# A graph-convolution kernel: loads and results issued from ScalarE, other places for the weight tiles and the packs' stores, and other PSUM buffers

## The chip, the core and the metric

The kernel runs on one core of one Trainium2 chip. The core has TensorE (PE; its weight loads are shown as PEld), VectorE (DVE), ScalarE (ACT), GpSimd (POOL) and SyncE (SP), each with an instruction stream of its own, executed in order. An engine that needs another's result waits on a semaphore. Transfers are issued from an engine's stream and run on 16 shared DMA engines. SyncE does nothing here but issue transfers. The time is the device time of one execution in microseconds, the median of several runs.

## The reference

There are 50,000 nodes with 160 features each (64 scalars s, and 32 vectors v of three components) and 1,650,000 edges, sorted by their destination; 50,000 of these are the loops from each node to itself. Each edge has four numbers sh = (e0, e1).

```python
ss, vv = (s[src], v[src])
e0, e1 = sh[:, 0:1], sh[:, 1:4]
dot = jnp.einsum('eui,ei->eu', vv, e1)
out0 = C0 * (ss * e0 @ W1 + dot * INV3 @ W2)
p3 = (ss @ W3)[:, :, None] * e1[:, None, :] * INV3
p4 = jnp.einsum('eui,uw->ewi', vv * e0[:, :, None], W4) * INV3
p5 = jnp.einsum('eui,uw->ewi', jnp.cross(vv, e1[:, None, :]), W5) * INV6
out1 = C1 * (p3 + p4 + p5)
m_agg = jax.ops.segment_sum(concat(out0, out1), dst, num_segments=n)
h = concat(m_agg_scalars @ Ws * LIN_S, m_agg_vectors @ Wv * LIN_V)
x = layernorm(x + (x + relu(h)))
```

All is linear in the features of the source node. So the kernel sums, for each node, the outer products of its edges' four numbers with the 160 source features, and multiplies the sums once by a combined weight.

## The kernel before

**Units, groups, pairs.** 128 edges make a unit, 6 units a group, 2 groups a *pair*: 12 units. There are 2,087 groups, so 1,044 pairs, and the outer loop at the end of the function runs over these. For each unit GpSimd issues one gather (L349): 128 rows of 640 bytes of x, chosen by the edges' sources, into one slot of the tile `xg`. `xg` holds a pair and has four buffers, so GpSimd can be four pairs ahead. The gathers stand in order of GpSimd's own stream and wait for the buffer they write.

**The weight tile.** For a pair VectorE builds `hot` (L358, which of 32 neighbouring destinations an edge has) and from it `ha` (L361, `hot` times the four numbers of the edge, 12 units of 128 columns) in `spread`. TensorE multiplies `ha` by the gathered rows (L386, in `group_sums`; each unit gives two weight loads and two matmuls) and adds the six units of a group in PSUM, in `ps`: 128 rows (4 numbers x 32 destinations) by 160 features for each of the two groups. `ps` has two buffers in the pool `psA`.

**Turning.** `turn_sums` transposes `ps` on VectorE into `sums` (L398) and adds it into `ring` (L405), the sums of the nodes of a segment of 512 nodes, at a place that is read into a register. When a segment begins, what two segments share is added (L402).

**The order of a pair.** The loop body issues the gathers of pair p and then walks the 12 units. After the matmuls of unit 1 comes `turn_sums` of pair p - 1; after those of unit 3 comes `spread` for pair p + 1; after every unit a bit of the tasks that are waiting (`work`) and some steps of the current pack. The program fixes this order on SyncE, TensorE, VectorE and ScalarE (`manual_schedule`).

**Tasks.** `after_pair(p, f)` hands a task over when pair p has been written. For a block of 128 nodes whose last group is in pair p: `do_ahead` at p loads `xt`, the block's own rows of x, two blocks with one transfer (L644); `do_block` at p + 2 multiplies the ring by the combined weight (L704, ten matmuls into `phb`, in the pool `psM`, tag "misc") and ends with relu, residual and statistics on VectorE (L182, L184, L186); `do_root` at p + 3 takes the root on ScalarE (L191, `rstd`); `do_store` at p + 4 takes the reciprocal and scales on VectorE (L195, L196); `do_send` at p + 6 stores two blocks (L784). There are 391 blocks, one in 2.7 pairs.

**Loads of edges.** 20 groups (10 pairs) form a chunk s. `load(s + 1)` is issued at the first pair of chunk s, `place` runs four pairs later: VectorE and TensorE find the first destination of each group (L318, L320, L322), transpose indices and numbers (L326 to L331) and make `si`, `rel` and `pk`, which `gather` and `spread` read. For the first 100 groups the edges are read from the inputs (L263 to L265). For all others they come from the tensor `edges` in DRAM (L257), from which the kernel has removed the loops.

**Packs.** That removal is the work of 16 packs of up to 128 rows of 790 edges. A pack is a list of steps: read the rows (L474 to L478), three empty steps, begin (copies on ScalarE, L482 to L484), counting and marking on VectorE with a copy by ScalarE (L502), shifting by predicated copies (L566), four empty steps, and 17 stores. A store step reads 16 addresses from SBUF into registers of SyncE and issues up to 16 transfers of 18.5 KB to `edges` and as many of 0.5 KB, the loops' numbers, to `selves` (L618). A pack has 77 steps, and the loop deals them evenly over the pairs from the end of the pack before to the pack's due time. The due times, by the planner, are the pairs 38, 99, 159, 229, 289 and so on to 989; the first pack begins at pair 2.

**The loops' share.** For each segment `ask_own` loads, six pairs before the segment begins, the nodes' own rows four times over (`xr`, L675, 640 KB) and their loops' numbers (`sr`, L676), twice 256 nodes a segment; `set_own` multiplies them and transposes them into the ring (L689, L693) at two pairs before.

**Queues.** In this version `dq` is SyncE, and every transfer of the main loop but the gathers is issued there: loads, packs' reads, packs' stores, xt, xr, sr and the results. An issue that has to wait holds up those after it.

Of the kernel before, what the change touches and what calls it, by code (L numbers as in the profile page):

```python
# [39 lines left out]
F32 = mybir.dt.float32  # L40
# [7 lines left out]
PSUM = bass.MemoryType.PSUM  # L48
# [54 lines left out]
def tile_gnn_resnorm(ctx: ExitStack, tc: tile.TileContext, x, src, dst, attr, W1, W2, W3, W4, W5, Ws, Wv, out, n_edges):  # L103
# [123 lines left out]
    with tc.tile_pool(name="once", bufs=1) as once, tc.tile_pool(name="raw", bufs=2) as rawp, \  # L227
# [2 lines left out]
            tc.tile_pool(name="ring", bufs=2) as ringp, tc.tile_pool(name="node", bufs=3) as np_, \  # L230
            tc.tile_pool(name="ahead", bufs=4) as aheadp, tc.tile_pool(name="outs", bufs=3) as outp, \
            tc.tile_pool(name="psC", bufs=1, space=PSUM) as psC, tc.tile_pool(name="psK", bufs=2, space=PSUM) as psK, \
            tc.tile_pool(name="psP", bufs=1, space=PSUM) as psP, tc.tile_pool(name="psA", bufs=2, space=PSUM) as psA, \
            tc.tile_pool(name="psM", bufs=2, space=PSUM) as psM, ExitStack() as later_pools:

        spotp, ownp = (later_pools.enter_context(tc.tile_pool(name=name, bufs=bufs))
                       for name, bufs in (("spot", 3), ("own", 2)))
# [6 lines left out]
        slotsP = bank[:, 0, :]  # L244
        nc.vector.tensor_copy(slotsP, slots)

        dq = nc.sync
        begun = []

        def load(s):  # L250

            g0 = s * SG
            n = (min(NG, g0 + SG) - g0) * G
            if g0 >= NH:
                p0 = g0 * G * P - EH
                r6 = rawp.tile([P, P, 2 + NK], F32, name="r6")
                dq.dma_start(r6[:n].rearrange("u p c -> u (p c)"),  # L257
                             edges[0, p0 * (2 + NK):(p0 + n * P) * (2 + NK)].rearrange("(u q) -> u q", u=n))
# [4 lines left out]
            dq.dma_start(ri[:n, 0, :], src1[e].rearrange("(u p) o -> u (p o)", p=P))  # L263
            dq.dma_start(ri[:n, 1, :], dst1[e].rearrange("(u p) o -> u (p o)", p=P))
            dq.dma_start(ra[:n].rearrange("u p k -> u (p k)"), attr[e].rearrange("(u p) k -> u (p k)", p=P))  # L265
            return s, n, ri, None, None, ra[:n]

        def cast(loaded):
# [102 lines left out]
        def fresh(kind):  # L371
            written[kind].append([])

        def wrote(kind, ins):
            ws = written[kind]
            for old in ws[-3] if len(ws) > 2 else []:
                tc.declare_no_dep(ins.ins, old, reason="its reader has waited for it")
            ws[-1].append(ins.ins)
            return ins

        def group_sums(p, rows, ha):

            ps = psA.tile([P, PG, D], F32, name="ps")
            fresh("ps")
            for j, xr in enumerate(rows):
                mm = nc.tensor.matmul(ps[:, j // G, :], ha[:, j].rearrange("p k w -> p (k w)"), xr,  # L386
                                      start=j % G == 0, stop=j % G == G - 1)
# [75 lines left out]
        def pack(c):  # L463
# [7 lines left out]
            def read():  # L471
                T["pri"] = pri = packp.tile([P, 2, L + 1], I32, name="pri")
                T["pra"] = pra = packp.tile([P, LW, NK], F32, name="pra")
                dq.dma_start(pri[:n, 0, :L], src1[e].rearrange("(r e) o -> r (e o)", e=L))  # L474
                dq.dma_start(pri[:n, 1, :L], dst1[e].rearrange("(r e) o -> r (e o)", e=L))

                dq.dma_start(pri[:n, 1, L:], dst1[e0 + L:e0 + L + n * L].rearrange("(r e) o -> r (e o)", e=L)[:, 0:1])
                dq.dma_start(pra[:n, :L].rearrange("r e k -> r (e k)"), attr[e].rearrange("(r e) k -> r (e k)", e=L))  # L478

            def begin():  # L480
                T["prow"] = rows = packp.tile([P, L + 1, C], F32, name="prow")
# [142 lines left out]


            for head, j in [(False, j) for j in range(RS)] + [(True, 0)]:
                steps.append(partial(store, head, j))
            return steps + [stored]

        def rows_of(b):  # L630
# [3 lines left out]
        def together(b):  # L634

            bs = list(range(b // BP * BP, min(nblocks, b // BP * BP + BP)))
            return bs if all(rows_of(i)[0] == P for i in bs) else [b]

        def ahead(bs):

            nb = rows_of(bs[0])[0]
            n0, n1 = rows_of(bs[0])[1].start, rows_of(bs[-1])[1].stop
            xt = aheadp.tile([P, BP, D], F32, name="xt")
            dq.dma_start(xt[:nb, :len(bs)], x[n0:n1, :].rearrange("(h n) d -> n h d", h=len(bs)))  # L644

            return [(xt[:, h],) for h in range(len(bs))]

# [13 lines left out]
        def ask_own(k, bs, got):  # L661

            n0, n1 = rows_of(bs[0])[1].start, rows_of(bs[-1])[1].stop
            assert rows_stored[0] == NR or row_start(rows_stored[0])[1][0] >= n1
            n = n1 - n0
            nq = next(q for q in range(math.ceil(n / W), n + 1) if n % q == 0)
            m = n // nq
            assert nq <= BP * P // W
            xr = ownp.tile([P, BP * P // W, D], F32, name="xr")
            sr = ownp.tile([P, BP * P // W], F32, name="sr")  # L670
            xs = x[n0:n1, :].rearrange("(w q) d -> w (q d)", q=nq).unsqueeze(0).to_broadcast([NK, m, nq * D])
            ss = selves[0, n0 * NK:n1 * NK].rearrange("(w q k) -> k w q", q=nq, k=NK)
            with nc.allow_non_contiguous_dma(reason="one number of each node"):
                if m == W:
                    dq.dma_start(xr[:, :nq].rearrange("p q d -> p (q d)"), xs)  # L675
                    dq.dma_start(sr[:, :nq], ss)  # L676
                else:
                    nc.vector.memset(xr[:, :nq], 0.0)
                    nc.vector.memset(sr[:, :nq], 0.0)
                    for k_ in range(NK):  # L680
                        r = slice(k_ * W, k_ * W + m)
                        dq.dma_start(xr[r, :nq].rearrange("p q d -> p (q d)"), xs[k_])
                        dq.dma_start(sr[r, :nq], ss[k_])
            got.extend((xr, sr, nq))

        def set_own(k, bs, got):
# [8 lines left out]
            if c0 + nq * W < c1:  # L695
                nc.vector.memset(ring[k][:, :, c0 + nq * W:c1], 0.0)

        def block(b, xt):
            nb, row = rows_of(b)
            k, c0 = b // SB, b % SB * P  # L700
            ph = psM.tile([P, D], F32, name="phb", tag="misc")
            fresh("misc")
            for i in range(ND):
                wrote("misc", nc.tensor.matmul(ph[:nb], ring[k][:, i, c0:c0 + nb], BWk[:, i, :],  # L704
                                               start=i == 0, stop=i == ND - 1))
                yield 1
            return norm1(np_, ph[:nb], xt[:nb], nb)
# [33 lines left out]
        def after_pair(p, f, *args):  # L741
            later.setdefault(p, []).append((f, args))
# [15 lines left out]
                else:  # L758
                    credit[0] -= cost

        of_nodes, resid, rstds, outs = {}, {}, {}, {}

        def do_ahead(b):
            bs = together(b)
# [1 line left out]
                of_nodes.update(zip(bs, ahead(bs)))  # L766

        def do_block(b):
            resid[b] = yield from block(b, *of_nodes.pop(b))

        def do_root(b):
            rstds[b] = norm2(np_, resid[b][1], rows_of(b)[0])
# [7 lines left out]
        def do_send(b):  # L780
            bs = together(b)
            if b == bs[-1]:
                n0, n1 = rows_of(bs[0])[1].start, rows_of(b)[1].stop
                dq.dma_start(out[n0:n1, :].rearrange("(h n) d -> n h d", h=len(bs)),  # L784
                             outs.pop(bs[0])[:rows_of(b)[0], :len(bs)])

        def do_cast(s):
# [268 lines left out]
```

## Time and profile before

| | |
|---|---|
| time, median of 3 runs | 17,993.06 us (17,989.49 to 18,003.85) |
| the profiled execution's own time | 18,022.17 us |
| its span, first to last instruction | 18,020.0 us |
| granted TensorE clock, mean | 0.625 |
| DMA traffic | 1,337 MB, 74 GB/s over the span |
| of it by the gathers' queue | 1,026.6 MB, 23.7% of the 16 engines' time |
| of it by SyncE's queue | 302.9 MB, 6.1% of the 16 engines' time |

The profile's groups carry the line of the kernel, the engine, the operation, the tile written and the tiles read. A row of the group list has the number of instructions, their busy time, the mean of one in ns, and the idle time of the engine before them with what ended most of it. In the waits, "A <- B" means that A was idle until B; "issue" means that nothing the profile shows was waited for, and "remote" a semaphore whose update came later than the instruction that is known to write it. In the timeline a line has the start, the duration, the engine and the instruction, and in brackets the idle time before it. In a count by stretches, the number after x is that of the instructions in the stretch. SyncE's issues carry a q (SPq).

### The profile page before, as it was taken

Reading aid. Unit: us, or ns where it says so; the run is one execution under the profiler, and the core shown is the slowest. Engines: PE = TensorE matmul, PEld = TensorE weight load, DVE = VectorE, ACT = ScalarE, POOL = GpSimd, SP = SyncE. Lnnn points to the kernel's source line nnn. Section 1 sums busy time; section 2 is a strip of 40 time slices with the busy share of each in tenths; the row PEclk is TensorE's granted clock in tenths of the full one; section 3 lists DMA queues with packets and bytes.
Section 4 is the critical chain, followed back from the end, with each engine's and each line's share of the span. In section 5 each row is a group of like instructions: output and inputs, shape, how many; then the busy total and the mean of one; then the engine's idle time right before and its main releaser. Section 6 shows DMA issues by size and latency. Waiting matters only on the chain. (4 is left out here: it accounts for less than half of the span.)

```text
span 18020.0 us, 99721 instructions
## 1 busy us (share of the span) xinstructions
PE 6879.0 (38%) x29811; PEld 6014.7 (33%) x29812; DVE 7032.6 (39%) x11269; ACT 227.8 (1%) x479; POOL 12137.8 (67%) x12535
## 2 busy tenths in 40 slices
PE   3333334343333333333333333334333333333333
PEld 3333333333333333333333333333333333333333
DVE  4343443434434343443433434344343433434332
ACT  0000000000000000000000000000000000000000
POOL 6666666666666666666666666666666666666666
PEclk6666666666666666666666666666666666666666
DMA  2222323232232322323223232322323223232222
GB/s 71 74 69 72 80 71 81 69 82 72 73 79 70 83 71 73 79 69 81 72 72 79 70 79 72 82 69 72 80 70 82 69 73 80 69 79 72 73 72 63
DMA packets 961715, 1337.18 MB, mean 74 GB/s; under 512 B 411739, under 2 KB 716048, under 8 KB 957182
## 3 DMA queue, kind: packets, MB, share of 16 engines
q0 software_dynamic: 601056, 1026.60, 23.7%
q1 hardware_dynamic: 358674, 302.87, 6.1%
q8 instruction: 238, 3.90, 0.1%
q14 instruction: 307, 2.51, 0.0%
q10 hardware_dynamic: 1440, 1.29, 0.0%
HBM read 1258.50 MB, written 71.40 MB: 74 GB/s over the span
## 5 line engine op out<-in xcount | busy, mean ns | idle before, releaser
L349 POOL DMA_INDIRECT xg<-in_x,si x12522 | 12134.1, 969 | 5859.5 <-issue 3666.1
L386 PE MATMUL ps<-xg,ha 128*128 128x160 f32 x25044 | 6255.4, 383 | 9081.8 <-issue 8146.9
L386 PEld LDWEIGHTS ps<-xg,ha 128*128 128x128 f32 x25044 | 5171.1, 254 | 9859.0 <-issue 8902.6
L398 DVE STREAM_TRANSPOSE sums<-ps 128x320 f32<-128x320 f32 x1044 | 529.7, 507 | 6341.5 <-remote 4050.5
L361 DVE TENSOR_TENSOR ha<-hot,pk 128x1536 f32<-128x1536 f32 x1044 | 1830.2, 1753 | 35.8
L182 DVE SCALAR_TENSOR_TENSOR y<-phb,xt 128x160 f32<-128x160 f32 x391 | 125.6, 321 | 3508.3 <-PE ps L386 1623.2
L704 PE MATMUL phb<-BWk,ring 128*128 128x160 f32 (+1 forms) x3910 | 1181.7, 388 | 454.0 <-issue 452.9
L704 PEld LDWEIGHTS phb<-BWk,ring 128*128 128x128 f32 (+1 forms) x3910 | 925.6, 266 | 470.0 <-issue 469.5
L405 DVE TENSOR_TENSOR ring<-ring,sums 128x160 f32 x2087 | 683.1, 327 | 309.7 <-issue 224.2
L358 DVE TENSOR_TENSOR hot<-bank,rel 128x384 f32<-128x384 f32 x1044 | 572.4, 548 | 107.0 <-remote 70.5
L693 DVE STREAM_TRANSPOSE ring<-xr 128x1280 f32<-128x1280 f32 x188 | 466.1, 2479 | 6.5
L566 DVE COPY_PREDICATED prow<-marks,prow 128x2370 f32<-128x2370 int32 (+8 forms) x160 | 445.4, 2784 | 1.1
L320 PE MATMUL bank<-first,ones 120*128 120x20 f32 (+1 forms) x210 | 59.4, 365 | 815.1 <-DVE first L318 573.0
L320 PEld LDWEIGHTS bank<-first,ones 120*128 120x128 f32 (+1 forms) x210 | 49.8, 292 | 853.6 <-DVE first L318 597.5
L191 ACT ACTIVATE rstd<-mv,eps_t 128x1 f32<-128x1 f32 x391 | 115.2, 295 | 17061.4 <-DVE st L184 5415.1
L326 PE MATMUL bank<-ident,r 120*128 120x120 f32 x100 | 46.2, 462 | 703.1 <-issue 361.0
L566 DVE COPY_PREDICATED pra<-marks,pra 128x1580 f32<-128x1580 int32 (+8 forms) x160 | 306.5, 1915 | 0.0
L689 DVE TENSOR_TENSOR xr<-xr,sr 128x1280 f32<-128x1280 f32 x188 | 277.0, 1473 | 57.4 <-DMA sr<-selves 35.9
L326 PEld LDWEIGHTS bank<-ident,r 120*128 120x128 f32 x100 | 21.1, 211 | 727.4 <-issue 369.7
L196 DVE TENSOR_SCALAR o<-y,mv,rstd 128x160 f32<-128x160 f32 x391 | 146.1, 374 | 19.6 <-issue 3.7
L402 DVE TENSOR_TENSOR ring<-ring 128x1280 f32<-128x1280 f32 x97 | 143.0, 1474 | 1.8
L331 PE MATMUL pk<-ident,r 120*128 120x120 f32 (+1 forms) x400 | 139.5, 400 | 0.0
(349 smaller groups left out, 2156.2 us busy)
## 6 DMA issues: line engine op xcount, KB each, us to landing
xg<-in_x,si POOLq DMA_INDIRECT x12522
xr<-in_x SPq DMA_DIRECT2D x187, 640.0 KB
edges<-prow SPq DMA_DIRECT2D x1994, 18.5 KB
r<-edges SPq DMA_DIRECT2D x99, 360.0 KB
selves<-mine SPq DMA_DIRECT2D x1992, 0.5 KB
xt<-in_x SPq DMA_DIRECT2D x195, 160.0 KB
out<-o SPq DMA_DIRECT2D x195, 160.0 KB
pra<-in_attr SPq DMA_DIRECT2D x15, 1580.0 KB
```

Source lines behind the costliest of these rows:

```text
L196: nc.vector.tensor_scalar(o[:n], y[:n], mv[:n, 0:1], rstd[:n], op0=ALU.subtract, op1=ALU.mult)
L349: nc.gpsimd.indirect_dma_start(out=xg[:, j, :], out_offset=None, in_=x, in_offset=bass.IndirectOffsetOnAxis(ap=placed[0][:, u + j:u + j + ...
L358: nc.vector.tensor_tensor(hot[:, :n], slotsP[:, 0:W].unsqueeze(1).to_broadcast([P, n, W]), rel[:, u:u + n].unsqueeze(2).to_broadcast([P, n ...
L361: nc.vector.tensor_tensor(ha[:, :n], hot[:, :n].unsqueeze(2).to_broadcast([P, n, NK, W]), pk[:, :, u:u + n].rearrange("p k u -> p u k").un ...
L386: mm = nc.tensor.matmul(ps[:, j // G, :], ha[:, j].rearrange("p k w -> p (k w)"), xr, start=j % G == 0, stop=j % G == G - 1)
L398: nc.vector.transpose(at[:, :ng], ps[:, :ng].rearrange("p g (b f) -> p g b f", f=FB))
L402: nc.vector.tensor_tensor(ring[k][:, :, :TW - S], ring[k][:, :, :TW - S], ring[k - 1][:, :, S:], op=ALU.add)
L405: nc.vector.tensor_tensor(here, here, at[:, i], op=ALU.add)
L566: nc.vector.copy_predicated(what[:n, a:e], mi[:, r].unsqueeze(2).to_broadcast([n, e - a, what.shape[2]]), what[:n, a + d:e + d])
L689: nc.vector.tensor_tensor(xr[:, :nq], xr[:, :nq], sr[:, :nq].unsqueeze(2).to_broadcast([P, nq, D]), op=ALU.mult)
L693: nc.vector.transpose(ring[k][:, :, c0:c0 + nq * W].rearrange("p b (w q) -> p q b w", q=nq), xr[:, :nq].rearrange("p q (b f) -> p q b f", ...
L704: wrote("misc", nc.tensor.matmul(ph[:nb], ring[k][:, i, c0:c0 + nb], BWk[:, i, :], start=i == 0, stop=i == ND - 1))
```

## The change

Six things change.

- A second name, `loads`, is ScalarE's queue. The edge loads (but the first), the packs' reads, xt, xr, sr and the results are issued there. SyncE keeps the packs' stores, the first load and the table of rows.
- Each store step of a pack is followed by two empty steps, so that a pack has 111 steps.
- `spread` for pair p + 1 moves from unit 3 to unit 0 of pair p, ahead of `turn_sums` of pair p - 1.
- The pool of `ps` has three buffers, that of `phb` one, and `wrote` leaves out the waits of `ps` on the buffer's earlier matmuls for the fourth tile back, of `phb` not at all.
- The sums of two blocks lie in one tile `phb` of 2 x 160 columns, taken at the first of the two.
- `do_ahead` is handed over three pairs earlier.

```diff
-            tc.tile_pool(name="psP", bufs=1, space=PSUM) as psP, tc.tile_pool(name="psA", bufs=2, space=PSUM) as psA, \
-            tc.tile_pool(name="psM", bufs=2, space=PSUM) as psM, ExitStack() as later_pools:
+            tc.tile_pool(name="psP", bufs=1, space=PSUM) as psP, tc.tile_pool(name="psA", bufs=3, space=PSUM) as psA, \
+            tc.tile_pool(name="psM", bufs=1, space=PSUM) as psM, ExitStack() as later_pools:
...
-        dq = nc.sync
+        dq, loads = nc.sync, nc.scalar
...
         def load(s):
+            q = loads if s else dq
...
-                dq.dma_start(r6[:n].rearrange("u p c -> u (p c)"),
+                q.dma_start(r6[:n].rearrange("u p c -> u (p c)"),
...
         def wrote(kind, ins):
             ws = written[kind]
-            for old in ws[-3] if len(ws) > 2 else []:
+            for old in ws[-4] if kind == "ps" and len(ws) > 3 else []:
                 tc.declare_no_dep(ins.ins, old, reason="its reader has waited for it")
...
             def read():
-                dq.dma_start(pri[:n, 0, :L], src1[e].rearrange("(r e) o -> r (e o)", e=L))
+                loads.dma_start(pri[:n, 0, :L], src1[e].rearrange("(r e) o -> r (e o)", e=L))
...
             for head, j in [(False, j) for j in range(RS)] + [(True, 0)]:
-                steps.append(partial(store, head, j))
+                steps += [partial(store, head, j), None, None]
             return steps + [stored]
...
-            dq.dma_start(xt[:nb, :len(bs)], x[n0:n1, :].rearrange("(h n) d -> n h d", h=len(bs)))
+            loads.dma_start(xt[:nb, :len(bs)], x[n0:n1, :].rearrange("(h n) d -> n h d", h=len(bs)))
...
-                    dq.dma_start(xr[:, :nq].rearrange("p q d -> p (q d)"), xs)
-                    dq.dma_start(sr[:, :nq], ss)
+                    loads.dma_start(xr[:, :nq].rearrange("p q d -> p (q d)"), xs)
+                    loads.dma_start(sr[:, :nq], ss)
...
-        def block(b, xt):
+        def block(b, xt, ph):
             nb, row = rows_of(b)
             k, c0 = b // SB, b % SB * P
-            ph = psM.tile([P, D], F32, name="phb", tag="misc")
-            fresh("misc")
...
         def do_block(b):
-            resid[b] = yield from block(b, *of_nodes.pop(b))
+            bs = together(b)
+            if b == bs[0]:
+                sums_of[b] = psM.tile([P, BP, D], F32, name="phb", tag="misc")
+                fresh("misc")
+            resid[b] = yield from block(b, *of_nodes.pop(b), sums_of[bs[0]][:, b - bs[0]])
...
-                dq.dma_start(out[n0:n1, :].rearrange("(h n) d -> n h d", h=len(bs)),
+                loads.dma_start(out[n0:n1, :].rearrange("(h n) d -> n h d", h=len(bs)),
...
-            after_pair(max(p, START - 1), do_ahead, b)
+            after_pair(max(p - 3, START - 1), do_ahead, b)
...
             for j, ps in enumerate(group_sums(p, rows, has.pop(p))):
+                if j == 0 and p + 1 < len(pairs):
+                    s1, g1, ng1 = pairs[p + 1]
+                    has[p + 1] = spread(placed[s1], (g1 - s1 * SG) * G, ng1 * G)
                 if j == 1 and turning:
                     turn_sums(*turning)
                     turning = None
-                if j == 3 and p + 1 < len(pairs):
-                    s1, g1, ng1 = pairs[p + 1]
-                    has[p + 1] = spread(placed[s1], (g1 - s1 * SG) * G, ng1 * G)
```

More of the change, by code (lines that the diff above doesn't have):

```diff
@@ L262, in load @@
             ra = rawp.tile([P, P, NK], F32, name="ra")
-            dq.dma_start(ri[:n, 0, :], src1[e].rearrange("(u p) o -> u (p o)", p=P))
-            dq.dma_start(ri[:n, 1, :], dst1[e].rearrange("(u p) o -> u (p o)", p=P))
-            dq.dma_start(ra[:n].rearrange("u p k -> u (p k)"), attr[e].rearrange("(u p) k -> u (p k)", p=P))
+            q.dma_start(ri[:n, 0, :], src1[e].rearrange("(u p) o -> u (p o)", p=P))
+            q.dma_start(ri[:n, 1, :], dst1[e].rearrange("(u p) o -> u (p o)", p=P))
+            q.dma_start(ra[:n].rearrange("u p k -> u (p k)"), attr[e].rearrange("(u p) k -> u (p k)", p=P))
             return s, n, ri, None, None, ra[:n]
@@ L473, in read @@
                 T["pra"] = pra = packp.tile([P, LW, NK], F32, name="pra")
-                dq.dma_start(pri[:n, 0, :L], src1[e].rearrange("(r e) o -> r (e o)", e=L))
-                dq.dma_start(pri[:n, 1, :L], dst1[e].rearrange("(r e) o -> r (e o)", e=L))
-                dq.dma_start(pri[:n, 1, L:], dst1[e0 + L:e0 + L + n * L].rearrange("(r e) o -> r (e o)", e=L)[:, 0:1])
-                dq.dma_start(pra[:n, :L].rearrange("r e k -> r (e k)"), attr[e].rearrange("(r e) k -> r (e k)", e=L))
+                loads.dma_start(pri[:n, 0, :L], src1[e].rearrange("(r e) o -> r (e o)", e=L))
+                loads.dma_start(pri[:n, 1, :L], dst1[e].rearrange("(r e) o -> r (e o)", e=L))
+                loads.dma_start(pri[:n, 1, L:], dst1[e0 + L:e0 + L + n * L].rearrange("(r e) o -> r (e o)", e=L)[:, 0:1])
+                loads.dma_start(pra[:n, :L].rearrange("r e k -> r (e k)"), attr[e].rearrange("(r e) k -> r (e k)", e=L))
             def begin():
@@ L681, in ask_own @@
                         r = slice(k_ * W, k_ * W + m)
-                        dq.dma_start(xr[r, :nq].rearrange("p q d -> p (q d)"), xs[k_])
-                        dq.dma_start(sr[r, :nq], ss[k_])
+                        loads.dma_start(xr[r, :nq].rearrange("p q d -> p (q d)"), xs[k_])
+                        loads.dma_start(sr[r, :nq], ss[k_])
             got.extend((xr, sr, nq))
@@ L759, in work @@
                     credit[0] -= cost
-        of_nodes, resid, rstds, outs = {}, {}, {}, {}
+        of_nodes, resid, rstds, outs, sums_of = {}, {}, {}, {}, {}
         def do_ahead(b):
```

## The prediction

> **What bounds the kernel now.** I read the page first, for the busy shares and the group of the gathers, then the waits, then counts of gathers in stretches of equal length, and last the timeline around the longest stops.
>
> ```profile
> PE 6879.0 (38%) x29811; PEld 6014.7 (33%) x29812; DVE 7032.6 (39%) x11269; ACT 227.8 (1%) x479; POOL 12137.8 (67%) x12535
> ...
> L349 POOL DMA_INDIRECT xg<-in_x,si x12522 | 12134.1, 969 | 5859.5 <-issue 3666.1
> ```
>
> GpSimd's 12,522 gathers are the one long row: 0.95 us each in the timeline with 0.30 us between two of them, so 1.254 us undisturbed, or 12,522 x 1.254 = 15,703 us of the 18,020. The remaining 2,300 us are stops of GpSimd (and some 260 us of gathers that ran long). The waits say who ends the stops:
>
> ```profile
> POOL xg L349 <- issue: 3666.1, 11991, 2.1
> ...
> POOL xg L349 <- PE ps L386: 1224.7, 236, 46.9
> POOL xg L349 <- remote: 875.2, 223, 7.0
> ...
> DVE y L182 <- DMA xt<-in_x: 241.7, 7, 93.1
> ```
>
> The first row is the 0.30 us between gathers. The next two are one thing, a semaphore of TensorE ("remote" is its late update): the four gather buffers are full and TensorE has not used the oldest. TensorE does not starve; by the instruction starts it stands 25 gathers behind GpSimd in the median. So is TensorE's chain the bound? Counting gathers in five quiet stretches:
>
> ```profile
> core 0: us, POOL busy (x), PEclk, DMA share, GB/s
> 2000.00:3000.00 1000.00, 675.30 (x700) 0.61 0.30 75
> 4000.00:5000.00 1000.00, 681.89 (x704) 0.61 0.30 75
> 9000.00:10000.00 1000.00, 671.66 (x697) 0.62 0.30 75
> 13000.00:14000.00 1000.00, 675.37 (x698) 0.63 0.31 76
> 17000.00:17900.00 900.00, 613.09 (x632) 0.62 0.29 70
> ```
>
> 697 to 704 per 1,000 us, everywhere: 1.428 us a gather, 17.14 us a pair of 12. The last stretch has almost no work of the packs, the others have all of it, and the pace is the same. I split TensorE's time, instruction start to instruction start, over 43 stretches of 24 pairs. Waits before a pair's first weight load (4.2 us a pair) and steps of over 0.6 us between instructions, most of 0.7 or 1.4 us and with nothing waited for (6.6 us a pair), replace each other with a correlation of -0.79: the stretch from pair 384 has 6.2 and 4.1 us and takes 17.06 us a pair, that from pair 840 has 2.3 and 9.6 and takes 17.20. Shorter waits were filled with slow steps, not turned into speed. The slow steps set in some 15 us after GpSimd restarts and end about when it stops, and runs of 24, 36 and 48 gathers between stops take 1.426, 1.424 and 1.430 us a gather, stop included. So I take 17.14 us a pair as a pace that waits of a few us do not change. What does change the time is a stop longer than the usual 4 to 6 us. There are 13 over 7 us; the largest are in these stretches:
>
> ```profile
> 625.00:875.00 250.00, 138.47 (x145) 0.59 0.31 82
> 8283.00:8502.00 219.00, 137.22 (x144) 0.60 0.35 90
> 10567.00:10786.00 219.00, 137.83 (x145) 0.61 0.34 86
> 16144.00:16364.00 220.00, 138.85 (x144) 0.62 0.30 74
> ```
>
> At 1.428 us these would take 207, 206, 207 and 206 us: 43, 13, 12 and 14 us too many, 82 in all. Their causes are loads that SyncE issued late:
>
> ```profile
> 849.76 0.48 SPq L644 DMA_DIRECT2D xt<-in_x  x1
> 850.28 0.51 SPq L257 DMA_DIRECT2D r<-edges  x1
> ...
> 852.04 14.99 SPq L675 DMA_DIRECT2D xr<-in_x  x1
> ```
> ```profile
> 8355.86 0.42 SPq L644 DMA_DIRECT2D xt<-in_x  x1
> 8358.78 0.32 DVE L182 SCALAR_TENSOR_TENSOR y<-phb,xt 128x160 f32<-128x160 f32 x1 [53.85 <-DMA xt<-in_x]
> ```
>
> In the second, VectorE stands 53.9 us for xt, and GpSimd 20.9. In the first, xt and the next edges (r) come behind pack 0's stores (522 to 809 us). At 10,640 it is a pack's own reads behind the previous pack's stores, at 16,137 xt again.
>
> **The change, part by part.** *Loads and results to ScalarE.* SyncE's issues of these, summed by line: r 145 us, the packs' reads 43, xt 95, xr 1,296, sr 127, results 179, in all 1,885 us; ScalarE goes from 228 to 2,110 us, 12% of the span. No transfer is added. Gone is the wait behind SyncE's 4,236 stores (1,519 us of issue, with as many register moves): the 82 us. New is that ScalarE's rstd (L191) and the packs' copies stand behind these issues. The second xr of a segment takes 12 to 16 us, over 10 us in 87 cases; behind ScalarE stand rstd, then VectorE's reciprocal (L195) and everything after it on VectorE. Cover: by the starts, the reciprocal comes 16 us after its statistics in the median, under 8.8 us in a quarter; and ScalarE, otherwise idle, issues xr when the last rstd is done, while two blocks are 48 us apart (34 or more in three of four). Bounds: 0 to 93 segments x 14 us = 1,300 us. I take 10 us, nearest to the row of block distances. The results' wait for o moves too (7,600 us of SyncE at L784); the o it waits for is two pairs old in VectorE's order, so rstd behind it loses nothing unless VectorE is late.
>
> By the Trainium skill (DMA: Bandwidth & Descriptors, Issuing engines are not separate DMA queues) transfers of all issuers run on the same 16 DMA engines, and another issuer saves only its issue time, usually small. By that rule alone this part would be worth nothing and the time 17,993; the rows of xt show lateness in the queue, and there I follow the rows.
>
> *Stores over more steps.* A pack has 59 steps of reading and VectorE work, 17 of stores, one end: 77; now 59 + 51 + 1 = 111. A pack has 60 pairs, the first 36. The stores need 258 to 396 us a pack (first to last issue), and had 17/77 of 60 pairs = 13 pairs = 227 us: too little, hence the late loads. Now 51/111 of 60 = 28 pairs = 470 us; for the first pack 16.5 pairs = 284 us against the 287 it took. VectorE's 1,923 us for 16 packs now fall in 53 instead of 77% of the pairs: 120 us in 32 pairs is 3.8 us a pair beside 5.2 of other work, 9 of 17.14. Cost 0, covered by VectorE's idle 8 us; without cover 1 to 2 us a pair.
>
> *xt three pairs earlier* costs nothing: four buffers, two in use. It takes the other cause of the 54 and 47 us waits away.
>
> *ha ahead of turning, a third ps, both blocks' phb in one bank.* No instruction is added; 8 banks before and after. VectorE builds ha one pair before TensorE can need it, so much of the 4.2 us before a pair can go. By the trade above it returns as slow steps: 0. Bounds: none, or all of GpSimd's stops (2,040 us). What I do count is runs of only 12 gathers between stops, 70 of them at 1.49 instead of 1.42 us: 70 x 12 x 0.07 = 59 us, of which a half, 30. The single phb bank makes a block's first matmul wait for the two blocks before it, the later of which ended two pairs ago: 0.
>
> **Sum**, against the profiled run's 18,020 us of span (its run 18,022.2; the three runs' median 17,993.1 is 29 us lower): -82 - 30 + 10 = -102, so 17,918, and 17,890 on the scale of the median.
>
> **Rivals.** *Late loads stay or new ones replace them*: the first pack's stores still need all of their 284 us, and ScalarE waits for results before it loads. Against it: half a pack more room in all later packs. A gain of 0 to 35 us, 17,958 to 18,029, middle 17,980; chance 0.2. *The loosened pair is real speed*: GpSimd's stops are ended by TensorE, which waits 4,387 us before first weight loads. Against it: the constant pace. A line through the runs between stops has a slope of 1.40 us a gather; at that 12,522 x 1.40 = 17,531, + 31 for both ends, 17,560, and 15,734 with no stop; chance 0.14 for anything under 17,800. *ScalarE becomes the late one*: place L675 on ScalarE, price up to 14 us for VectorE in each of 93 segments, decisive once about 12 segments pay 10 us in VectorE's burst after a stop, when a pair takes 5 to 9 us instead of 17. A quarter of them (the short reciprocals) at 10 us: +230, 18,120; chance 0.18, slower. The rest, 0.48, is my forecast, its own range 17,800 to 17,957.
>
> **How the numbers follow.** Likeliest 17,890. The range of 17,640 to 18,090 cuts off most of the fast rival and the worst of ScalarE. A change of 0.2% (36 us) is about what a measurement tells from none. Faster 0.48 + 0.14 = 0.62, same 0.20, slower 0.18.
>
> **What would show it.** Right: 700 gathers per 1,000 us outside long stops; no wait of y for xt over 10 us; no stop over 20 us near 820; waits before first weight loads shorter and slow steps more. ScalarE's rival: VectorE idle before L195, now never. Wrong altogether if quiet stretches hold over 715 gathers, or under 690.

## The result and the profile after

The changed kernel is slower: 19,051.97 us (median of 4 runs, 19,040.46 to 19,099.75) against 17,994.65 us for the kernel before on the same chip, a ratio of 1.0592 with a 95% interval of 1.0573 to 1.0611. The forecast was 17,890, in a range of 17,640 to 18,090.

First the page of the changed kernel, the busy row and the gathers:

```profile
PE 6997.6 (37%) x29811; PEld 5898.8 (31%) x29812; DVE 7028.4 (37%) x11269; ACT 224.6 (1%) x479; POOL 12158.7 (64%) x12535
...
L350 POOL DMA_INDIRECT xg<-in_x,si x12522 | 12155.0, 971 | 6864.6 <-issue 3666.6
```

The engines work about as long as before: VectorE 7,028 against 7,033 us, TensorE's matmuls 119 us more and its weight loads 116 us less. The gathers are as long as they were. GpSimd's idle time ahead of them went from 5,859.5 to 6,864.6 us: 1,005 of the 1,027 us that the span grew (18,020.0 to 19,046.7). The waits say what ended it, and what is new beside it (engine, line and releaser; us in all, times, the longest):

```profile
POOL xg L350 <- issue: 3666.6, 12009, 1.6
...
POOL xg L350 <- PE ps L387: 2274.8, 211, 95.1
...
ACT prow L483 <- DMA edges<-prow: 1323.0, 13, 184.9
...
DVE hit L504 <- ACT marks L503: 1169.4, 15, 137.6
...
POOL xg L350 <- remote: 788.9, 166, 11.3
...
DVE rstd L195 <- ACT rstd L191: 605.3, 5, 141.4
```

GpSimd's longest stop has doubled, from 46.9 to 95.1 us. Three rows are new or were next to nothing. ScalarE's copy into `prow`, the first act of a pack, waits up to 184.9 us for the stores of the pack before (`edges<-prow`; `prow` has one buffer). VectorE's first count of a pack (`hit`, L504) waits for ScalarE's copy `marks`, fifteen times (6.9 us in all before), and its reciprocal (L195) for ScalarE's rstd, five times: 1,775 us in which VectorE does nothing. The wait of y for xt (241.7 us before) is not among the rows any more.

As a stop I count what the starts of two gathers in a row are further apart than 1.254 us, where that is over 1 us; so some gathers that ran long are in the sums. There are exactly fifteen stops over 15 us, one for each pack but the first, at pairs 46, 107, 167, 237 and so on to 937; each is 67 to 95 us long, 1,191 us in all. The other stops sum to 2,037 us; before, all stops summed to 2,195. So the loss is one event a pack, and the rest of the kernel became a little faster. Three of the same stretches as before show it:

```profile
core 0: us, PE busy (x) PEld busy (x) DVE busy (x) ACT busy (x) POOL busy (x), PEclk, DMA share, GB/s
2000.00:3000.00 1000.00, 391.57 (x1678) 329.51 (x1676) 390.76 (x624) 6.19 (x21) 675.82 (x697) 0.62 0.29 74
4000.00:5000.00 1000.00, 356.43 (x1511) 306.60 (x1511) 377.07 (x589) 12.36 (x25) 616.07 (x635) 0.60 0.26 69
9000.00:10000.00 1000.00, 393.16 (x1724) 333.97 (x1724) 392.20 (x628) 6.48 (x22) 680.70 (x703) 0.62 0.28 72
```

The stretches without a pack's begin hold 697 and 703 gathers, as before; the one with a begin (4,361 us) holds 635, which is 65 gathers or 93 us fewer than the mean of these two, at 1.428 us.

One begin, that of pack 7, on ScalarE (start, duration, engine and line; in brackets the idle time and what ended it):

```profile
7660.03 0.35 ACTq L475 DMA_DIRECT2D pri<-in_src  x1
...
7661.40 0.44 ACTq L479 DMA_DIRECT2D pra<-in_attr  x1
7839.57 0.35 ACTq L258 DMA_DIRECT2D r<-edges  x1
7839.95 0.42 ACTq L645 DMA_DIRECT2D xt<-in_x  x1
7845.14 1.58 ACT L483 CAST prow<-pri 128x790 f32<-128x790 int32 x1 [184.88 <-DMA edges<-prow]
...
7850.93 0.48 ACT L503 CAST marks<-pri 128x395 f32<-128x395 int32 x1
```

ScalarE issues the pack's reads at 7,661, then stands 178 us at the load of `r` and some more at the copy. Its next work is at 7,845, and `marks` at 7,851. VectorE meanwhile, and GpSimd around it:

```profile
7740.00:7780.00 40.00, 3.04 (x23) 2.80 (x21) 0.00 (x0) 0.00 (x0) 30.25 (x33) 0.58 0.27 74
7780.00:7864.00 84.00, 5.12 (x24) 4.91 (x24) 12.15 (x22) 6.56 (x6) 1.12 (x2) 0.51 0.08 24
```

VectorE is idle from 7,739; GpSimd fills its buffers for another 42 us (33 gathers in 40 us), and in the next 84 us it starts one more (the other of the two in the count began before).

What SyncE does in that time is the last stores of pack 6. Of pack 1's 272 stores it had issued 41 when ScalarE asked for pack 2 (1,802 us), though the steps deal them evenly up to there; the other 231 came by 1,975. Their order shows why. A program built from the kernel gives each transfer one of eight semaphores in turn, over both queues together, and each transfer waits until the one before it on that semaphore has landed, unless its engine has seen that already. The turns follow the order in which the recording layer (what makes a program of the kernel's calls) puts the transfers, and that need not be the program's. From the changed kernel's built order (place, number in the program's order, engine, line, its semaphore and count, target):

```
4732  5122  SP   L619  2:832  selves      4794  5124  SP   L619  5:832  selves
4737  5123  SP   L619  3:832  edges       4795  7062  ACT  L476  6:832  pri
4787  7061  ACT  L475  4:832  pri         4798  5125  SP   L619  7:832  edges
```

Store 5124 was written some 1,900 instructions ahead of the read 7061 and stands behind it. In the fifteen packs that have a successor 223 to 253 of the 272 stores stand behind the next pack's read. So a store waits for whatever ScalarE has eight places ahead of it (xt, results, xr, sr), ScalarE issues that when it gets there, and the stores run late by a whole read. The waits of SyncE's stores in the changed kernel name these transfers:

```profile
SPq L619 <- DMA sr<-selves: 591.6, 15, 172.4
...
SPq L619 <- DMA xr<-in_x: 511.2, 11, 165.9
...
SPq L619 <- DMA xt<-in_x: 235.2, 9, 62.5
```

### The profile page after: what moved, and what is told of

It reads as the page before. It is cut to its first block, busy times and chain, and to the rows that moved or that the text cites. A ratio compares the mean times of both kernels' runs of the same rounds, so it can differ in the third digit from the quotient of the medians.

```text
span 19046.7 us, 99772 instructions
## 1 busy us (share of the span) xinstructions
PE 6997.6 (37%) x29811; PEld 5898.8 (31%) x29812; DVE 7028.4 (37%) x11269; ACT 224.6 (1%) x479; POOL 12158.7 (64%) x12535
## 5 line engine op out<-in xcount | busy, mean ns | idle before, releaser
L350 POOL DMA_INDIRECT xg<-in_x,si x12522 | 12155.0, 971 | 6864.6 <-issue 3666.6
L387 PEld LDWEIGHTS ps<-xg,ha 128*128 128x128 f32 x25044 | 5070.4, 248 | 9952.9 <-issue 9077.5
L703 PEld LDWEIGHTS phb<-BWk,ring 128*128 128x128 f32 (+1 forms) x3910 | 876.3, 249 | 1101.5 <-issue 1100.0
L504 DVE TENSOR_TENSOR hit<-marks,prow 128x395 f32<-128x395 f32 (+1 forms) x32 | 26.9, 842 | 1177.2 <-ACT marks L503 1169.4
L195 DVE RECIPROCAL rstd<-rstd 128x1 f32<-128x1 f32 x391 | 60.9, 156 | 626.8 <-ACT rstd L191 605.3
```

The lines of the kernel that those rows point to most:

```text
L350: nc.gpsimd.indirect_dma_start(out=xg[:, j, :], out_offset=None, in_=x, in_offset=bass.IndirectOffsetOnAxis(ap=placed[0][:, u + j:u + j + ...
```

## The experiments

Two kinds of chips came up. On the first, where the result above is from, the kernel before takes 17,994 to 18,138 us; on the second it takes 15,972 to 15,982. Every ratio below is to the kernel before on the same chip.

| run | kernel | before, us | time, us | ratio, 95% interval |
|---|---|---|---|---|
| e1 | changed, all transfers on SyncE | 18,118 | 18,028.5 | 0.9949 [0.9932, 0.9965] |
| e2 | before, loads and results on ScalarE | 18,118 | 19,162.6 | 1.0571 [1.0553, 1.0589] |
| e3 | changed, stores one a step | 18,118 | 19,157.0 | 1.0573 [1.0555, 1.0591] |
| e4 | changed, only xt and results on ScalarE | 18,118 | 18,773.6 | 1.0355 [1.0338, 1.0372] |
| e5 | changed, queues in the program's order | 15,972 | 15,966.5 | 0.9996 [0.9987, 1.0005] |
| e6 | before, stores dealt over more steps | 15,972 | 15,984.1 | 1.0007 [0.9998, 1.0016] |
| e7 | ha, ps and phb of the change alone | 15,972 | 15,969.2 | 0.9998 [0.9989, 1.0007] |
| e8 | before | 15,972 | 15,980.8 | one run |
| e9 | changed | 15,982 | 16,004.7 | 1.0014 [1.0005, 1.0023] |
| e10 | as e5 | 15,982 | 15,975.6 | 0.9996 [0.9987, 1.0005] |
| e11 | as e6 | 15,982 | 15,994.0 | 1.0009 [1.0000, 1.0018] |
| e12 | as e7 | 15,982 | 15,982.2 | 0.9999 [0.9990, 1.0008] |
| e13 | changed, two buffers of rows | 17,994 | 19,063.9 | 1.0590 [1.0567, 1.0613] |
| e14 | as e5, two buffers of rows | 17,994 | 17,975.7 | 0.9990 [0.9980, 0.9999] |
| e15 | changed | 17,994 | 19,047.0 | 1.0582 [1.0555, 1.0608] |
| e16 | as e5 | 17,994 | 17,932.4 | 0.9961 [0.9947, 0.9975] |
| e17 | as e6 | 18,138 | 18,082.9 | 0.9971 [0.9961, 0.9982] |
| e18 | as e7 | 18,138 | 18,104.8 | 0.9985 [0.9976, 0.9994] |

### Which part of the change

e1, the changed kernel on one queue:

```diff
-        dq, loads = nc.sync, nc.scalar
+        dq, loads = nc.sync, nc.sync
```

> The changed kernel with every load and result issued by SyncE again; the rest of the change (stores dealt over three times the steps, ha ahead, third ps buffer, earlier xt) stays. Theory A (the two queues are tied together: SyncE's stores wait for ScalarE's loads, run out late, and the next pack's first copy into the single prow buffer waits on ScalarE for them, with VectorE behind it): the fifteen stops of GpSimd of 67 to 95 us, one a pack, go, 1,191 us in all; time 17,800 to 17,950, ScalarE's prow copy waits no longer than the 61 us of before. Theory B (the dealing itself ends the stores too late for the next pack, whoever issues the loads): the stops stay, 18,900 to 19,100. Theory C (ScalarE's own issue time, xr's 12 to 16 us ahead of rstd): 17,800 to 17,950 as A.

e2, the other way round: the kernel before with `dq` turned into `loads = nc.scalar` at each of the change's loads and results, nothing else.

> The kernel before with only the loads and results moved to ScalarE; stores one a step, ha, PSUM and xt as before. Theory A: a long stop of GpSimd at each pack's begin, 60 to 100 us each, time 18,900 to 19,300. Theory B: no such stops, 17,880 to 18,000. Theory C: 18,100 to 19,000 with many stops of 5 to 20 us where xr is asked for, and none tied to the packs.

e3 keeps the queues of the changed kernel and takes the dealing back:

```diff
-                steps += [partial(store, head, j), None, None]
+                steps.append(partial(store, head, j))
```

> The changed kernel with its stores one a step again (77 steps to a pack), loads on ScalarE. Theory A: the stops stay, 18,900 to 19,200. Theory B: they go, 17,800 to 17,950. Theory C: 19,050 as the changed kernel.

e1 has no stop over 15 us and is 0.5% faster than before; e2 and e3 have a long stop at each pack and lose 5.7%. The dealing (theory B) is out: without it the stops stay, with it on one queue they are absent. The move to ScalarE makes the loss alone. It is not ScalarE's issue time (theory C) either: e2's sixteen stops over 15 us (34 us at pair 996, 63 to 98 at the others) come once a pack, where C had many of 5 to 20 us. e1's 18,028.5 is outside the 17,800 to 17,950 that was expected, since this chip is 0.7% slower for the kernel before too; the ratio is what can be compared.

e4 leaves only transfers on ScalarE that share no data with the stores:

```diff
-        dq, loads = nc.sync, nc.scalar
+        dq, loads, nodes = nc.sync, nc.sync, nc.scalar
...
-            loads.dma_start(xt[:nb, :len(bs)], x[n0:n1, :].rearrange("(h n) d -> n h d", h=len(bs)))
+            nodes.dma_start(xt[:nb, :len(bs)], x[n0:n1, :].rearrange("(h n) d -> n h d", h=len(bs)))
...
-                loads.dma_start(out[n0:n1, :].rearrange("(h n) d -> n h d", h=len(bs)),
+                nodes.dma_start(out[n0:n1, :].rearrange("(h n) d -> n h d", h=len(bs)),
```

> The changed kernel with only the blocks' xt loads and out results on ScalarE; the packs' reads, r, xr and sr on SyncE again. Theory A: in the built order the stores no longer stand behind the next pack's read (0 of 272, where 225 to 235 of 272 do in the changed kernel), so no stop at the packs' begin: 17,780 to 17,930. Theory B: 18,900 to 19,100. Theory C: 17,800 to 17,950, since xr is off ScalarE.

All three theories missed: 1.0355. SyncE's waits of e4, and then VectorE's:

```profile
SPq L619 <- DMA xt<-in_x: 1197.6, 24, 107.4
...
SPq L619 <- DMA out<-o: 259.4, 18, 103.2
```
```profile
DVE xr L690 <- DMA sr<-selves: 1236.1, 45, 82.7
DVE first L319 <- DMA r<-edges: 426.2, 15, 48.6
```

The stores wait for xt and for results, which are data that they neither read nor write. So the shared semaphores tie the queues even where the order of stores and reads is right. Theory A had counted only the packs' reads: in e4's built order 4,402 of SyncE's 4,799 transfers still stand behind a transfer of ScalarE that the program has later (4,165 of 4,241 in the changed kernel, none in that of e5 below). And as SyncE also has xr, sr and r here, these come late behind the held stores, and VectorE waits for them. In 25 stops of 18 to 56 us GpSimd loses 773 us. The price of the tie comes out wherever something stands behind it.

### The order alone

e5 leaves every engine's instructions and their order as they are in the changed kernel, and adds edges that carry no wait, so that the two queues take their turns at the semaphores in the program's order:

```diff
+            def dma_start(self, *args):
+                ins = self.engine.dma_start(*args)
+                if self.other in latest:
+                    tc.add_manual_dep(ins.ins, latest[self.other],
+                                      mybir.DependencyInfo(mybir.DependencyClass.NoSync, mybir.DependencyReason.SCHED_ONLY),
+                                      reason="in the order of the program")
+                latest[self.engine is nc.sync] = ins.ins.name
+                return ins
...
-        dq, loads = nc.sync, nc.scalar
+        dq, loads = InOrder(nc.sync, False), InOrder(nc.scalar, True)
```

> The changed kernel with the loads and results still on ScalarE; the only edit is an edge from each transfer of SyncE or ScalarE to the latest transfer that the program issued on the other one, so that the built order of the two queues is the program's (in the changed kernel 225 to 235 of a pack's 272 stores stand behind the next pack's read; here none). Every engine's own instructions and their order are unchanged. Theory A1 (the transfers of both queues take turns at eight semaphores in the built order, and each waits for the one eight places ahead; the built order is what makes the stores late): the fifteen long stops go, ratio to before 0.985 to 0.998. Theory A2 (what binds is the data: r and sr have to wait for the stores that wrote them, whatever the order): the stops stay, 1.04 to 1.06. Theory A3 (two queues on shared semaphores wait for each other in any order): part of it stays, 1.005 to 1.035.

e5 came onto a chip of the second kind, where by itself it told nothing. It ran again beside the changed kernel, twice:

> The changed kernel itself, beside the three that follow. On a chip where the kernel before takes about 18,000 us: 1.057 to 1.061, fifteen stops. On a chip where it takes about 15,970: theory A (SyncE's stores run out late by the built order and hold ScalarE, and VectorE behind it, for some 150 us a pack) has VectorE's wait at each pack's begin there too, and GpSimd stops for what of it the six buffers of rows do not cover: 16,500 to 17,200, ratio 1.03 to 1.08. If the stops come only where TensorE steps slowly: 1.000 to 1.01.

> The changed kernel with the two queues in the program's order. Theory A1 (built order): 0.990 to 1.000 on either kind of chip, no stop of GpSimd over 25 us. Theory A2 (data): as the changed kernel. Theory A3: halfway, 1.01 to 1.04 where the kernel before takes 18,000 us.

> The changed kernel, beside e16 on the same chip. Where before takes 18,000 us: 1.055 to 1.062. Where it takes 15,980: 1.000 to 1.003.

> The changed kernel with the two queues in the program's order, loads still on ScalarE. Where before takes 18,000 us, theory A1 (built order): 0.990 to 1.000, no stop of GpSimd over 25 us; theory A3 (any order on shared semaphores): 1.01 to 1.04. Where before takes 15,980: 0.999 to 1.001.

On one chip of the first kind the changed kernel takes 19,047.0 us and the same kernel with the queues in order 17,932.4: 1,114.5 us from the order alone, with 1.0582 against 0.9961 of the kernel before. The largest stop of GpSimd in e16 is under 15 us, and TensorE's longest hold on it 13.5 us (95.1 in the changed kernel). In e10 and e16 the lines from the queues' definition on are shifted by 16, and the transfers of both queues have that of the helper, L255:

```profile
POOL xg L366 <- PE ps L403: 1136.0, 206, 13.5
POOL xg L366 <- remote: 853.3, 188, 9.8
```

Theory A1 holds; A2 (data) and A3 (any order on shared semaphores) do not, as far as the price goes. The tie itself is still there: SyncE's transfers wait for ScalarE's in e16 too, at most 53 us at a time, and nothing that stops GpSimd for long stands behind them:

```profile
SPq L255 <- DMA xt<-in_x: 308.7, 18, 52.7
SPq L255 <- DMA xr<-in_x: 202.4, 14, 39.5
```

On the second kind of chip the same cause is in the traces, at hardly any price. Pack 7's begin on ScalarE, of e9 and then of e10:

```profile
6395.12 0.44 ACTq L479 DMA_DIRECT2D pra<-in_attr  x1
6503.54 0.35 ACTq L258 DMA_DIRECT2D r<-edges  x1
...
6510.66 1.58 ACT L483 CAST prow<-pri 128x790 f32<-128x790 int32 x1 [116.67 <-DMA edges<-prow]
```
```profile
6394.86 0.44 ACTq L255 DMA_DIRECT2D pra<-in_attr  x1
6395.39 0.39 ACTq L255 DMA_DIRECT2D r<-edges  x1
...
6397.20 1.59 ACT L499 CAST prow<-pri 128x790 f32<-128x790 int32 x1 [3.66 <-DMA pri<-in_src]
```

108 us between the pack's last read and `r` became 0.5, and the copy's wait 3.7. VectorE's waits for `marks` and rstd are 724.5 and 318.6 us in e9. In e10 the two come to 10.1 and nothing. Yet e9 is only 29 us slower than e10, with four stops of 3 to 9 us, far from the 16,500 to 17,200 that theory A expected of e9; its ratio of 1.0014 lies in the other range, 1.000 to 1.01. (The expectation speaks of six buffers of rows; the kernel has four.)

### Why the same order costs 1,115 us on one chip and 29 on another

e13 and e14 are the changed kernel and e5 with the gathered rows in two buffers in place of four:

```diff
-            tc.tile_pool(name="idx", bufs=2) as idxp, tc.tile_pool(name="rows", bufs=4) as rowp, \
+            tc.tile_pool(name="idx", bufs=2) as idxp, tc.tile_pool(name="rows", bufs=2) as rowp, \
```

> The changed kernel with two buffers of gathered rows in place of four, so 24 gathers of cover (30 us at 1.254 us each) and not 48. Cover theory: on a chip where before takes 15,980 us, VectorE's waits of 50 to 79 us at thirteen packs now stop GpSimd for 20 to 50 us each: 16,250 to 16,650, ratio 1.017 to 1.042. If the rows' buffers do not matter there: 16,000 to 16,050. On a chip where before takes 18,000: 19,100 to 19,800.

> The kernel with the two queues in the program's order and two buffers of gathered rows. Cover theory: without the packs' waits the two buffers suffice where before takes 15,980 us: 15,970 to 16,080, ratio 0.999 to 1.007, so that nearly all that e13 loses is the built order's. If two buffers are too few by themselves: as e13. On a chip where before takes 18,000: 18,000 to 18,700, under e13 by 800 to 1,300.

They came onto a chip of the first kind. e13 is as slow as the changed kernel (1.0590 against 1.0582), and e14 loses 43 us to e16, so all of e13's loss is the order's again. But the question they were made for stays open: the lag of TensorE behind GpSimd shrank with the buffers, from 21 to 3 gathers in the median, so that what is left to fill is much the same: 48 - 21 = 27 gathers (34 us) with four buffers, 24 - 3 = 21 (26 us) with two. The stops did not become longer (62 to 98 us), and both times lie just under what was expected, e13's by 36 us and e14's by 24.

What can be said for the second kind is arithmetic, not an experiment. In e9 TensorE stands 3 gathers behind, so 45 gathers or 56 us are free to fill. The waits of VectorE there are shorter too, at most 79 us for `marks` against 138. SyncE's stores follow each other faster: 0.53 us apart in the mean against 0.93 in the changed kernel of the first chip (spacings under 5 us). Waits of 48 to 79 us against 56 leave at most 23, where 3 to 9 were seen; 101 to 141 against some 35 leave 66 to 106, where 67 to 95 were seen. That the cover makes the difference is not shown.

### What the rest of the change is worth

The remaining runs split the 0.4 to 0.5% that is gained once the queues do no harm. e8 is the kernel before, for its profile; it met a chip of the second kind, and with 15,980.8 us, against 18,000 to 18,130 expected, and no stop over 3 us it was the first sight of what the last section tells. e6 and e7 (and e11, e12) ran on the second kind of chip, and again as e17 and e18 on the first. e6 is the kernel before with `[partial(store, head, j), None, None]`; e7 is e1 with the stores one a step and `do_ahead` at `max(p, START - 1)`.

> The kernel before, all transfers on SyncE, with only the stores dealt over three times the steps. If the dealing makes the 0.5% that the changed kernel gains on one queue: 0.993 to 0.997. If ha ahead and the third ps buffer make it: 0.999 to 1.002.

> The changed kernel with all transfers on SyncE, the stores one a step and xt asked for as before: what is left of the change is ha built at the pair's first step, three ps buffers and one phb bank. By the prediction's claim that waits of a few us cost nothing: 0.999 to 1.001. If these make the 0.5%: 0.993 to 0.997. If the one phb bank costs: over 1.002.

> The kernel before, unchanged, for a profile on the same chip: by all theories 18,000 to 18,130 with three stops of GpSimd over 15 us, as in the first profile.

> The kernel before with only the stores dealt over three times the steps. Where the kernel before takes 18,000 us: 0.993 to 0.997 if the dealing makes the 0.5% of the one-queue kernel, 0.999 to 1.002 if not. Where it takes 15,970: 1.000 to 1.001.

> The changed kernel on one queue with the stores one a step and xt as before, so ha ahead, three ps and one phb bank alone. Where the kernel before takes 18,000 us: 0.993 to 0.997 if these make the 0.5%, 0.999 to 1.001 if waits of a few us cost nothing. Where it takes 15,970: 0.999 to 1.001.

> The kernel before, all transfers on SyncE, with only the stores dealt over three times the steps. Where before takes 18,000 us: 0.994 to 0.997 and no stop of GpSimd over 15 us if the late loads behind dense stores were the loss that the change takes away; 0.999 to 1.001 if not. Where it takes 15,980: 1.000 to 1.002.

> The changed kernel on one queue with the stores one a step and xt as before: ha ahead, three ps buffers and one phb bank alone. Where before takes 18,000 us: 0.999 to 1.001 by the prediction's claim that waits of a few us cost nothing; 0.994 to 0.998 if these make the gain. Where it takes 15,980: 0.999 to 1.001.

On the first kind the dealing gives, by the ratio, 0.29% (53 us, interval 33 to 71; just outside the range expected of e17) and takes all the stops over 15 us away. ha, ps and phb give 0.15% (27 us, 11 to 44), between the two ranges that were expected of e18; their kernel still has the 43 us stop at pair 45, behind pack 0's dense stores. Neither does anything on the second kind, where GpSimd has no stops to lose; the dealing even costs 0.07 to 0.09% there, just at the edge of what those intervals resolve. The best kernels are the changed one on one queue (e1, 0.9949) or with its queues in order (e16, 0.9961). Their intervals overlap, so moving the loads to ScalarE gains nothing that was measured even when it is done well.

## Why the prediction was wrong, step by step

**The bound and the pace: right, for the kind of chip it was read from.** GpSimd's gathers and their stops are the time, and the quiet stretches of the changed kernel hold 697 to 703 gathers, within the 690 to 715 that were named. That waits of a few us do not set the pace held but for a remainder: the waits before a pair's first weight load fell from 4,387 us to 3,038 in the changed kernel, 1,359 in e16 and 1,543 with ha, ps and phb alone (e18), steps of 0.35 to 2.2 us from the start of an instruction to that of a matmul into ps rose from 3,236 us to 3,901, 4,266 and 4,089, and e18, with some 2,800 us of such waits less, is 27 us faster. What the prediction called a pace was not the kernel's, though: on the second kind of chip the kernel before runs at 1.254 us a gather and has no such steps at all.

**Loads and results to ScalarE, +10 us: the step that failed.** The prediction priced the move by the time that the issues take on ScalarE (xr's 12 to 16 us ahead of rstd), and bounded it with 1,300 us. It saw that the packs' copies stand behind the issues too, but gave that no price. It never asked what a transfer waits for once its neighbours in time are issued by another engine. On one queue the store before and the load after follow each other in any case; on two, each can become a wait of one engine on the other. Measured, the move alone costs 1,045 us (e2 less the kernel before), and in the changed kernel the order that the move brought costs 1,114.5 (e15 less e16): inside the bound by chance, since neither the place with a price (the begin of a pack, L258 and L483, not xr at L675) nor the releaser (SyncE's stores) was named. The trace of before could not show the new order; the built order of the changed program could, as soon as it existed.

**The 82 us of late loads: right in cause, smaller in size.** On one queue the dealing removes the stops and gains 53 us; the forecast had them go by the new queue, and there they were replaced by worse. "No stop over 20 us near 820" was wrong: the changed kernel stops 82.5 us at 793.

**Stores over more steps, cost 0.** The room was there (in e16 a pack's stores take 445 to 577 us from the second pack on, and hold nobody up), and VectorE's denser packs cost nothing: e17 is faster than before. But "28 pairs, 470 us" took the steps' places for the times of the stores. On two queues 41 of 272 kept to them in pack 1.

**ha, ps and phb, -30 us; xt, 0.** 27 us, and the waits of y for xt are gone. That the size fits is luck as far as is known: the -30 was to come from runs of only 12 gathers between stops, and with stops over 2 us these are 19 in the profile of before and 29 in e18. Where the 27 us come from is open.

**The sum and the rivals.** The forecast of 17,890, which has only 10 us for the failed step, is 0.9943 of the median before; without that step's loss e1 measured 0.9949 and e16 0.9961. The rival that had ScalarE become the late one named the right engine, and VectorE idle at L195 as its sign, which came (605.3 us). Its price of 230 us was from the wrong waits, as above, and 0.18 was little for a mechanism with a bound of 1,300 us. That the Trainium skill (DMA: Bandwidth & Descriptors, Issuing engines are not separate DMA queues) values another issuer at its issue time alone agrees with e16 against e1 (0.9961 and 0.9949, intervals that overlap). The loss came from the waits between the two issuers.

## What to carry to other kernels

Before moving transfers from one queue to another, list what each of them waits for in the built program, its semaphore's previous user included: a transfer that shares nothing with another one can still wait for it. An engine that computes should not stand in line behind a transfer that may wait; here, at pack 7, 42 us of buffered work hid less than a half of VectorE's 113 us of standing. And when two queues are wanted, look at the order in which the program's transfers were laid out, not only at each engine's own order: an edge without a wait was worth 5.9%.

## What the runs showed of the hardware that was not expected

The same program has two paces on different chips: 17,994 to 18,138 us and 15,972 to 15,982, 11 to 12% less. It is not TensorE's granted clock, which is 0.625 in the slower profile and 0.576 in the faster. The rows of the kernel before on a chip of the second kind (e8):

```profile
9000.00:10000.00 1000.00, 657.83 (x1857) 428.53 (x1856) 460.24 (x709) 13.99 (x30) 761.70 (x783) 0.58 0.35 84
```
```profile
L349 POOL DMA_INDIRECT xg<-in_x,si x12522 | 12130.8, 969 | 3824.9 <-issue 3552.3 <-PE ps L386 217.2 <-DMA xg<-in_x,si 39.1
L386 PE MATMUL ps<-xg,ha 128*128 128x160 f32 x25044 | 9923.5, 507 | 5282.0 <-DMA xg<-in_x,si 5125.9 <-DVE ha L361 34.0 <-DVE sums L398 18.1
```

783 gathers in 1,000 us instead of 697: GpSimd's stops, counted as above, sum to 200 us, not 2,195, and nearly all of the 200 is gathers that ran long. Its idle time before the gathers is 3,825 us, not 5,860, and most of what is left is the 0.30 us between two. TensorE waits for the rows to land, and no matmul into ps starts 0.35 to 2.2 us after the start of the instruction ahead of it; on the first kind 3,236 us go into such steps. SyncE is slow on the first kind too: in the changed kernel pack 6's last stores come mostly 1.4 to 2.8 us apart while GpSimd gathers, and mostly 0.32 us apart from 7,787 us on, some 6 us after its last gather. What slows the other engines' instructions while GpSimd gathers on these chips is open, and it is not the buffers' depth alone: e14, with TensorE 3 gathers behind, has less than a third of the steps of e16 (1,164 against 4,266 us) and its pace but for 0.2%, so these steps alone do not set the pace either.
